# A spectral convolution kernel: exponent tables and mirror differences moved between stages and engines

## The chip, the cores and the metric

The kernel runs on one core of one Trainium2 chip. The metric is the device time of the whole program in microseconds; the three runs shown before the change have a median of 2677.54 us (2671.09 to 2678.12). Engines are named as in the profile: PE (TensorE, matrix products; PEld is its weight load), DVE (VectorE), ACT (ScalarE), POOL (GpSimd) and SP (SyncE, which here only issues transfers). [...]

## The reference, cut to what matters

The input x is 16 images of 16 channels, 256 x 256, in float32. Two layers follow each other, each a group normalization (`_gn`), a convolution and a residual sum:

```python
x = x + _L0_conv_ref(_gn(x), L0_conv_weight)          # 3x3 circular convolution
x = x + _L1_conv_ref(_gn(x), ty, tx, pole1, pole2, residue)

# _L1_conv_ref, cut
alpha = fft2(x)
A = 1 / (omega1 - pole1);  Bm = 1 / (omega2 - pole2)
S = einsum('ikpq,oikp,xikq->oxik', residue, A, Bm)
output_residue1 = einsum('biox,oxik->bkox', alpha, S)
output_residue2 = einsum('bikpq,ikpq->bkpq', D, residue)  # D: alpha with A and Bm
x1 = ifft2(output_residue1).real
E1 = exp(pole1[..., None] * ty);  E2 = exp(pole2[..., None] * tx)
F = einsum('kbpq,bipz->kbiqz', output_residue2, E1)
x2 = einsum('kbiqz,biqx->kizx', F, E2).real
return x1 + x2 / Nx / Ny
```

The exponentials E1 and E2 depend on the poles and coordinates only, not on x. They are wanted in the last stage alone, for x2.

## The kernel before, in words

The work goes through four stages, with all large intermediates in DRAM between them.

1. **Convolution** (lines 107 to 665, span 0 to about 618 us). A loop over g runs 384 steps and three more, 24 steps for each image b: `conv(g)` issues 32 small matmul records into four accumulators `ps_conv`. Every sixth step a pair of row groups is finished: ScalarE evicts it to `vt` (L280), and `mirror` (L230) then takes the two mirrored halves `lo` and `hi`, makes their sum in `vsum` (L232) and their difference in place in `lo` (L235), both on VectorE. `square` (L240) makes the squares with running sums on ScalarE, and SP stores sum and difference as `vD` (L292). The three lists `later`, `squared` and `folded` hold work back to a step number: mirror at g + 2, squares at g + 4 and g + 5, stores at g + 3, where g is the step of the last eviction of the pair. Statistics of x for the images ahead (`x_stats`: bn_stats on VectorE, small matmuls L178, weights `wc`) and x loads (L123, at steps 3 and 15 of an image) run in between.

   Two chains of generators make tables beside it, one piece every 2 or 4 steps: `make_poles`, `make_hat` twice and `make_c` on the one, `make_exps` twice and `make_coef` on the other.

   `make_exps(which)` makes E1 or E2 as real tables in eight pairs q. For a pair: `th` = t times the pole's imaginary part (GpSimd, L490), `ex` = Exp of t times its real part (ScalarE, L491), a rounding of the angle to turns with a large constant (`rn`, GpSimd, L492 to L495), the reduction of the angle in three steps (VectorE, L501) and clamping (L504, L505), Sin (ScalarE, L507), the product with `ex` and the sum and difference of mirrored halves (GpSimd, L509, L511), and the store to `eD` (SP, L516), twice for E1 and once for E2. Each alternation of Exp and Sin loads an activation table (ACT_TABLE_LOAD).

2. **Transform along y and x** (line 668 on, about 618 to 1243 us): v is read back, folded by VectorE and GpSimd, and multiplied with the tables; the spectrum goes to `aD`. Unchanged.

3. **Mixing** (lines 868 to 1131, about 1243 to 1910 us). For each of 32 groups g of frequencies and each of four steps n: `sums` (L981) makes the mixing weights for g + 1 into two banks `ps_s`; `spread` copies each bank into `sg`, half by ScalarE (L996) and half by VectorE's stream_shuffle (L997); `mix` (L1063) makes four banks `ps_mix`, three emptied into `yt` by ScalarE and the fourth by VectorE (both L1120). `load(g + 1, n)` then fetches the part of `aD` for the next g (nothing for n = 0; L1045 for n = 1; L1050 for n = 2, 3), and `store(g, n, yt)` (L1077) writes four transfers to `yD`. There are two `yt` buffers. `weights` (L918) prepares the factors for g + 2 in three pieces on VectorE (L926 to L942), and for a last product `w` on GpSimd (L952), in the step n = 2.

4. **Inverse transform and output** (line 1134 on, about 1910 to 2677 us): reads `yD`, `eD` (`et`, `ey`) and v, and writes the result. Unchanged.

Within a stage the order on each engine is the order of the code (`manual_schedule`). A pool with one buffer (`bufs` 1) lets a tile of the same tag be written again only when its last reader, a transfer included, is done.

Of the kernel before, what the change touches and what calls it, by code (L numbers as in the profile page):

```python
# [17 lines left out]
C = 16  # L18
# [6 lines left out]
def conv_then_laplace_kernel(ctx: ExitStack, tc: tile.TileContext, a: dict, out: bass.AP):  # L25
# [84 lines left out]
    vp = p1.enter_context(tc.tile_pool(name="vt", bufs=4))  # L110
# [119 lines left out]
    def mirror(g, b, u, lo, hi):  # L230
        both = fp.tile([P, 2, 2, N], FP, name="vsum", tag="vsum")
        nc.vector.scalar_tensor_tensor(  # L232
            both, lo, 1.0, hi, ALU.mult, ALU.add, accum_out=sums[:, b, u : u + 1]
        )
        nc.vector.tensor_tensor(lo, lo, hi, ALU.subtract)  # L235
        folded.append((g + 3, b, u, (both, lo)))
        squared.append((g + 4, lambda: square(both, 4 + 2 * u, b, bias=shift2[:, b : b + 1])))
        squared.append((g + 5, lambda: square(lo, 5 + 2 * u, b)))
# [211 lines left out]
    def make_coef():  # L450


        rs = sw.tile([P, C, 4, 2], FP, name="s_rs", tag="s_th")
# [3 lines left out]
        u = sw.tile([P, 4, C, 4], FP, name="s_u", tag="s_rn")  # L457
# [14 lines left out]

    def make_exps(which):


        pl = sw.tile([P, C, 2], FP, name="s_pl", tag="s_pl")
        nc.sync.dma_start(out=pl, in_=a[f"pole_e{which + 1}"])
        t = sw.tile([P, N], FP, name="s_t", tag="s_t")
        nc.sync.dma_start(out=t, in_=a[("ty", "tx")[which]].to_broadcast([P, N]))
        sign, phase, turns = (cols[:, 2 + 3 * which + j : 3 + 3 * which + j] for j in range(3))  # L480
        pim = sw.tile([P, C], FP, name="s_pim", tag="s_pim")
        nc.vector.tensor_scalar(pim, pl[:, :, 1], sign, None, ALU.mult)
        yield
        for q in range(8):
            th = sw.tile([P, 2, N], FP, name="s_th", tag="s_th")
            rn = sw.tile([P, 2, N], FP, name="s_rn", tag="s_rn")
            ex = sw.tile([P, 2, N], FP, name="s_ex", tag=f"s_ex{q % 2}")
            for j in range(2):
                i = 2 * q + j
                nc.gpsimd.tensor_scalar(th[:, j], t, pim[:, i : i + 1], None, ALU.mult)  # L490
                nc.scalar.activation(ex[:, j], t, AF.Exp, scale=pl[:, i, 0:1])  # L491
            nc.gpsimd.tensor_scalar(rn, th, 1.0 / (2 * PI), turns, ALU.mult, ALU.add)  # L492
            magic = 1.5 * 2.0**23
            nc.gpsimd.tensor_scalar(rn, rn, magic, None, ALU.add)
            nc.gpsimd.tensor_scalar(rn, rn, magic, None, ALU.subtract)  # L495
            yield
            c1 = 6.28125
            c2 = float(np.float32(1.93500518798828125e-3))
            c3 = 2 * np.pi - c1 - c2
            for c in (c1, c2, c3):  # L500
                nc.vector.scalar_tensor_tensor(th, rn, -float(c), th, ALU.mult, ALU.add)  # L501
                if c == c2:
                    yield
            nc.vector.tensor_scalar(th, th, phase, 3.1415925, ALU.add, ALU.min)  # L504
            nc.vector.tensor_scalar(th, th, -3.1415925, None, ALU.max)  # L505
            yield
            nc.scalar.activation(th, th, AF.Sin)  # L507
            yield
            nc.gpsimd.tensor_tensor(th, th, ex, ALU.mult)  # L509
            for op, eo in ((ALU.add, 0), (ALU.subtract, 1)):  # L510
                nc.gpsimd.tensor_tensor(  # L511
                    ex[:, :, eo * P : eo * P + P], th[:, :, 0:P], th[:, :, N - 1 : P - 1 : -1], op
                )
            yield
            for o in range(2 - which):
                nc.sync.dma_start(  # L516
                    out=eD[which][o, :, 2 * q : 2 * q + 2].rearrange("p i e t -> p i (e t)"),
                    in_=ex,
                )
# [114 lines left out]
    for b in range(1, B):  # L634
# [4 lines left out]
        (4, 1, chain(make_exps(0), make_exps(1), make_coef())),  # L639
# [234 lines left out]
    kp0 = pool(p2, "spare")  # L874
# [19 lines left out]
    kp0.tile([P, 2304], FP, name="spare", tag="spare")  # L894
# [208 lines left out]

    p2.enter_context(tc.manual_schedule())
# [3 lines left out]
    unmix = None  # L1108
    for g in range(32):
# [3 lines left out]
        for n in range(4):  # L1113
            evict = sums(n, w_now) if ahead is not None else []
            yt = yp.tile([P, 2, 4 * B, 16], FP, name="yt", tag="yt")
            for odd, ps in enumerate(evict):
                spread(ahead, n, odd, ps.rearrange("p q n -> p n q"))
            for m in range(4):
                o, src = mix(4 * n + m, sg, yt)
                (nc.vector.tensor_copy if m == 3 else nc.scalar.copy)(o, src)  # L1120
            if g < 31:
                load(g + 1, n)
            store(g, n, yt)
            if n == 1 and unmix is not None:
                next(unmix, None)
                unmix = None
            wt = next_step(steps, None) or wt
        if g == 2:
            unmix = unmix_first()
            next(unmix)  # L1130
    p2.close()
# [360 lines left out]
```

## Time and profile before

| | |
|---|---|
| median of 3 runs | 2677.54 us |
| profiled execution, its own time | 2679.43 us |
| its span | 2677.6 us |
| mean granted TensorE clock | 0.982 |
| busy: PE, PEld, DVE, ACT, POOL | 2508.3, 1861.7, 2029.9, 1480.2, 1014.6 us |
| chain that ended last, by engine | PE 59%, DVE 12%, DMA 11%, POOL 5%, issue 5%, ACT 4%, SPq 4% |
| groups of the chain | ps_mix L1063 11%, ps_y L730 9% and L738 8%, DMA yD<-yt 4%, ps_conv L265 4% |
| ACT COPY yt L1120 (384) | busy 203.9 us, idle before it 214.8 us |
| DVE differences L235 (64) | busy 89.2 us, mean 1393 ns |
| POOL w L952 (32) | busy 60.9 us, idle before it 534.0 us |

Busy time is the union of an engine's instructions. A group's idle time is what its engine did nothing in before these instructions, with the releaser that ended most of it. The chain is followed backward from the last instruction, at each step to what released it. The granted clock and the transfer share (mean busy share of the 16 DMA engines) are given for each stretch in the tables by windows.

### The profile page before, as it was taken

How to read it: one execution, taken by the hardware profiler on the slowest of the kernel's cores; microseconds unless marked ns; L12 is line 12 of the kernel's file. 1: busy time of each engine (PE TensorE's matmuls, PEld its weight loads, DVE VectorE, ACT ScalarE, POOL GpSimd, SP SyncE). 2: the span in 40 equal slices, each digit the busy share in tenths (PEclk: the TensorE clock that was granted, in tenths of full speed). 3: DMA queues.
4: the chain of work that ended last, by engine and by line, in shares of the span. 5: the costliest groups of instructions: out<-in, count | busy, mean ns of one | idle time of the engine just before them, and what ended most of it. 6: DMA issues, size and time to landing. Idle time of an engine off the chain costs nothing.

```text
span 2677.6 us, 84178 instructions
## 1 busy us (share of the span) xinstructions
PE 2508.3 (94%) x35376; PEld 1861.7 (70%) x35376; DVE 2029.9 (76%) x3774; ACT 1480.2 (55%) x2772; POOL 1014.6 (38%) x988
## 2 busy tenths in 40 slices
PE   5888899898999999997989999999799999999998
PEld 2333444455777777774778888888678888888887
DVE  7777798967888888887777878787267666766666
ACT  4666687775666666664545555566334444444443
POOL 1333476612333333333200101010456565565753
PEclk9999999998999999998999999999899999999999
DMA  8777688855665666565667777777789899898995
GB/s 302 263 270 247 239 302 280 285 194 174 240 223 204 215 238 220 203 221 206 188 199 217 226 220 229 219 229 222 220 285 290 282 288 284 285 290 286 291 287 179
DMA packets 462729, 652.23 MB, mean 244 GB/s; under 512 B 49336, under 2 KB 425144, under 8 KB 448400
## 3 DMA queue, kind: packets, MB, share of 16 engines
q1 hardware_dynamic: 461280, 639.65, 73.6%
q8 instruction: 279, 4.57, 0.7%
q0 software_dynamic: 928, 3.02, 0.4%
q10 hardware_dynamic: 144, 4.19, 0.4%
q14 instruction: 98, 0.80, 0.1%
HBM read 367.22 MB, written 279.50 MB: 242 GB/s over the span
## 4 chain that ended last, share of the span: by engine, by line
PE 59%; DVE 12%; DMA 11%; POOL 5%; issue 5%; ACT 4%; SPq 4%; DVEq 0%; ACTq 0%; POOLq 0%
PE ps_mix L1063 11%; PE ps_y L730 9%; PE ps_y L738 8%; PE ps_p L1246 6%; PE ps_f L1270 5%; PE ps_f L1271 5%; PE ps_x L773 4%; DMA yD<-yt 4%; PE ps_conv L265 4%; PE ps_s L981 3%; DMA out_y<-ol 3%; DMA yk<-yD 2%; DVE xst L166 2%; SPq L1077 2%; DVE r L1279 2%
## 5 line engine op out<-in xcount | busy, mean ns | idle before, releaser
L1063 PEld LDWEIGHTS ps_mix<-abd,sg 128*64 128x64 f32 x8192 | 450.9, 138 | 74.3 <-ACT yt L1120 55.8
L1063 PE MATMUL ps_mix<-abd,sg 128*64 128x128 f32 x8192 | 481.9, 276 | 20.8 <-ACT yt L1120 20.6
L265 PE MATMUL ps_conv<-xt,wc 32*32 32x512 f32 x12288 | 459.0, 608 | 28.9 <-issue 17.7
L1210 POOL TENSOR_TENSOR u<-yk 128x512 f32<-128x512 f32 (+1 forms) x268 | 348.4, 1331 | 311.1 <-PE ps_p L1246 197.8
L746 ACT ACTIVATE t<-ps_y,vmr 128x384 f32<-128x384 f32 x512 | 298.1, 582 | 158.9 <-PE ps_y L738 158.8
L265 PEld LDWEIGHTS ps_conv<-xt,wc 32*32 32x32 f32 x12288 | 223.1, 104 | 216.7 <-issue 127.6
L997 DVE STREAM_SHUFFLE sg<-ps_s 128x512 f32<-128x512 f32 (+1 forms) x264 | 326.0, 1325 | 0.0
L1120 ACT COPY yt<-ps_mix 128x512 f32<-128x512 f32 x384 | 203.9, 600 | 214.8 <-DMA yD<-yt 174.5
L730 PE MATMUL ps_y<-tabE,vq 128*128 128x256 f32 x1024 | 313.5, 388 | 9.4 <-DVE vq L719 7.8
L738 PE MATMUL ps_y<-tabO,vq 128*128 128x256 f32 x1024 | 306.3, 381 | 0.0
L1270 PE MATMUL ps_f<-pt,inv 128*128 128x256 f32 x1008 | 300.6, 380 | 0.0
L1271 PE MATMUL ps_f<-hs,ey 128*128 128x256 f32 x1008 | 299.8, 379 | 0.0
L1246 PEld LDWEIGHTS ps_p<-inv,u 128*128 128x128 f32 x2048 | 265.6, 193 | 42.2 <-issue 24.7
L1274 DVE TENSOR_TENSOR r<-ps_f,q 128x256 f32<-128x256 f32 x256 | 107.0, 418 | 246.6 <-ACT q L1273 246.6
L1246 PE MATMUL ps_p<-inv,u 128*128 128x128 f32 x2048 | 279.1, 280 | 4.9 <-POOL u L1214 4.9
L952 POOL TENSOR_TENSOR w<-v,mcol 128x1024 f32<-128x1024 f32 x32 | 60.9, 1902 | 534.0 <-DVE v L942 534.0
L1273 ACT COPY q<-ps_f 128x256 f32<-128x256 f32 x256 | 95.6, 373 | 286.3 <-PE ps_f L1271 284.1
L730 PEld LDWEIGHTS ps_y<-tabE,vq 128*128 128x128 f32 x1024 | 189.8, 191 | 85.9 <-ACT q L786 50.3
L280 ACT ACTIVATE vt<-ps_conv,xq 128x512 f32<-128x512 f32 x256 | 160.6, 683 | 117.1 <-PE ps_conv L265 116.6
L1248 ACT COPY pt<-ps_p 128x512 f32<-128x512 f32 x256 | 150.5, 588 | 130.7 <-PE ps_p L1246 126.1
L738 PEld LDWEIGHTS ps_y<-tabO,vq 128*128 128x128 f32 x1024 | 195.7, 191 | 27.0
L1271 PEld LDWEIGHTS ps_f<-hs,ey 128*128 128x128 f32 x1008 | 191.5, 190 | 26.0
(232 smaller groups left out, 3822.6 us busy)
## 6 DMA issues: line engine op xcount, KB each, us to landing
xt<-in_x SPq DMA_DIRECT2D x31, 2322.0 KB, 9.6
yD<-yt SPq DMA_DIRECT2D x512, 128.0 KB, 3.2
vl<-vD SPq DMA_DIRECT2D x256, 256.0 KB, 3.8
out_y<-ol SPq DMA_DIRECT2D x128, 512.0 KB, 9.8
s<-vD SPq DMA_DIRECT2D x252, 256.0 KB, 6.4
aD<-spec SPq DMA_DIRECT2D x15, 4096.0 KB, 12.6
yk<-yD SPq DMA_DIRECT2D x60, 1024.0 KB, 8.3
vD<-vsum SPq DMA_DIRECT2D x128, 256.0 KB, 4.5
```

Source lines behind the costliest of these rows:

```text
L265: nc.tensor.matmul(acc[r][32 * c : 32 * c + 32], lhsT=ready[b][0][rows, phase, tap], rhs=halves[b][u // 2][rows, q : q + 5 : 4, 2 - tap : ...
L280: nc.scalar.activation(vt[:, r % 2], acc[r], AF.Identity, bias=ready[b][1])
L730: nc.tensor.matmul(ps[:, 0:N], lhsT=vf[:, xo, 0, j], rhs=tabE[:, 0 : i + 2 : i + 1], start=True, stop=False, skip_group_check=True,)
L738: nc.tensor.matmul(ps[:, P : P + N], lhsT=vf[:, xo, 1, j], rhs=tabO[:, i : C + 1 : C - i], start=False, stop=True, skip_group_check=True,)
L746: nc.scalar.activation(t[:, xo, j].rearrange("p l n -> p (l n)"), ps[:, 0:384], AF.Copy, scale=vmr[:, 0, b0 + j, i : i + 1],)
L997: nc.vector.stream_shuffle(to[..., C + k : C + k + 2], src, swap)
L1063: nc.tensor.matmul(ps[64 * t : 64 * t + 64, j], lhsT=sg[:, f : f + 2].rearrange("p f m -> p (f m)"), rhs=abd[jq][:, :, 2 * t + cc, 2 * jj ...
L1120: (nc.vector.tensor_copy if m == 3 else nc.scalar.copy)(o, src)
L1210: nc.gpsimd.tensor_tensor(u[:, :, j].rearrange("p b (c n) -> p c b n", c=8), in0, in1, o)
L1246: nc.tensor.matmul(ps[:, at], lhsT=u[:, n], rhs=tab, start=True, stop=True)
L1270: nc.tensor.matmul(ps[:, e], lhsT=tab, rhs=pt[:, e], start=True, stop=False)
L1271: nc.tensor.matmul(ps[:, e], lhsT=ey[:, e], rhs=hs, start=False, stop=True)
```

## The change

Three things are done.

- In `mirror` the difference of the halves goes from VectorE to GpSimd. The square of the sum is queued at g + 5 in place of g + 4, that of the difference at g + 7 in place of g + 5, and the stores of both at g + 6 in place of g + 3. The pool of `vt` has six buffers in place of four.
- `make_exps` leaves the convolution and runs in the mixing stage, one piece a step from g = 1 on. Its work on VectorE (three angle steps, clamping and the small product `pim`) is now on GpSimd, where a fused multiply and add becomes a product in `tmp` and a subtraction. All its tiles, `ex` among them, have one buffer, in a pool that stands where a spare tile stood. It has one more `yield`, after the store. `make_coef` alone remains in the second chain of the convolution, with tags of its own.
- In the mixing stage a step's `store` is issued before the next group's `load`.

```diff
-    vp = p1.enter_context(tc.tile_pool(name="vt", bufs=4))
+    vp = p1.enter_context(tc.tile_pool(name="vt", bufs=6))
...
-        nc.vector.tensor_tensor(lo, lo, hi, ALU.subtract)
-        folded.append((g + 3, b, u, (both, lo)))
-        squared.append((g + 4, lambda: square(both, 4 + 2 * u, b, bias=shift2[:, b : b + 1])))
-        squared.append((g + 5, lambda: square(lo, 5 + 2 * u, b)))
+        nc.gpsimd.tensor_tensor(lo, lo, hi, ALU.subtract)
+        folded.append((g + 6, b, u, (both, lo)))
+        squared.append((g + 5, lambda: square(both, 4 + 2 * u, b, bias=shift2[:, b : b + 1])))
+        squared.append((g + 7, lambda: square(lo, 5 + 2 * u, b)))
...
-        (4, 1, chain(make_exps(0), make_exps(1), make_coef())),
+        (4, 1, make_coef()),
...
-    kp0 = pool(p2, "spare")
+    ep = pool(p2, "exps")
...
+    def make_exps(which):
+        pl = ep.tile([P, C, 2], FP, name="s_pl", tag="s_pl")
+        nc.sync.dma_start(out=pl, in_=a[f"pole_e{which + 1}"])
+        t = ep.tile([P, N], FP, name="s_t", tag="s_t")
+        nc.sync.dma_start(out=t, in_=a[("ty", "tx")[which]].to_broadcast([P, N]))
...
+        nc.gpsimd.tensor_scalar(pim, pl[:, :, 1], sign, None, ALU.mult)
+        yield
+        for q in range(8):
...
+            ex = ep.tile([P, 2, N], FP, name="s_ex", tag="s_ex")
+            for j in range(2):
+                i = 2 * q + j
+                nc.gpsimd.tensor_scalar(th[:, j], t, pim[:, i : i + 1], None, ALU.mult)
+                nc.scalar.activation(ex[:, j], t, AF.Exp, scale=pl[:, i, 0:1])
+            nc.gpsimd.tensor_scalar(rn, th, 1.0 / (2 * PI), turns, ALU.mult, ALU.add)
+            magic = 1.5 * 2.0**23
+            nc.gpsimd.tensor_scalar(rn, rn, magic, None, ALU.add)
+            nc.gpsimd.tensor_scalar(rn, rn, magic, None, ALU.subtract)
+            yield
...
+            for c in (c1, c2, c3):
+                nc.gpsimd.tensor_scalar(tmp, rn, float(c), None, ALU.mult)
+                nc.gpsimd.tensor_tensor(th, th, tmp, ALU.subtract)
+                if c == c2:
+                    yield
+            nc.gpsimd.tensor_scalar(th, th, phase, 3.1415925, ALU.add, ALU.min)
+            nc.gpsimd.tensor_scalar(th, th, -3.1415925, None, ALU.max)
+            yield
+            nc.scalar.activation(th, th, AF.Sin)
+            yield
+            nc.gpsimd.tensor_tensor(th, th, ex, ALU.mult)
+            for op, eo in ((ALU.add, 0), (ALU.subtract, 1)):
+                nc.gpsimd.tensor_tensor(
+                    ex[:, :, eo * P : eo * P + P], th[:, :, 0:P], th[:, :, N - 1 : P - 1 : -1], op
+                )
+            yield
+            for o in range(2 - which):
+                nc.sync.dma_start(
+                    out=eD[which][o, :, 2 * q : 2 * q + 2].rearrange("p i e t -> p i (e t)"),
+                    in_=ex,
+                )
+            yield
...
+    exps = chain(make_exps(0), make_exps(1))
     for g in range(32):
...
+            store(g, n, yt)
             if g < 31:
                 load(g + 1, n)
-            store(g, n, yt)
...
             wt = next_step(steps, None) or wt
+            if g:
+                next(exps, None)
...
+    for _ in exps:
+        pass
```

More of the change, by code (lines that the diff above doesn't have):

```diff
@@ L450, in make_coef @@
     def make_coef():
-        rs = sw.tile([P, C, 4, 2], FP, name="s_rs", tag="s_th")
+        rs = sw.tile([P, C, 4, 2], FP, name="s_rs", tag="s_rs")
         nc.sync.dma_start(out=rs, in_=a["res_kq"])
@@ L456, in make_coef @@
         yield
-        u = sw.tile([P, 4, C, 4], FP, name="s_u", tag="s_rn")
+        u = sw.tile([P, 4, C, 4], FP, name="s_u", tag="s_u")
         m0, m1 = cols[:, 0:1], cols[:, 1:2]
@@ L471, in make_coef @@
         yield
[L473 to L519, printed above, removed]
     def make_c():
@@ L893, in conv_then_laplace_kernel @@
     ]
-    kp0.tile([P, 2304], FP, name="spare", tag="spare")
     zp.tile([P, 384], FP, name="between", tag="between")
@@ L1100, in unmix_first @@
             nc.sync.dma_start(out=at[:, c], in_=t[:, c])
+    def make_exps(which):
[3 more added lines that the diff above has]
+        nc.sync.dma_start(out=t, in_=a[("ty", "tx")[which]].to_broadcast([P, N]))
+        sign, phase, turns = (cols[:, 2 + 3 * which + j : 3 + 3 * which + j] for j in range(3))
+        pim = ep.tile([P, C], FP, name="s_pim", tag="s_pim")
+        nc.gpsimd.tensor_scalar(pim, pl[:, :, 1], sign, None, ALU.mult)
+        yield
+        for q in range(8):
+            th = ep.tile([P, 2, N], FP, name="s_th", tag="s_th")
+            rn = ep.tile([P, 2, N], FP, name="s_rn", tag="s_rn")
+            tmp = ep.tile([P, 2, N], FP, name="s_tmp", tag="s_tmp")
+            ex = ep.tile([P, 2, N], FP, name="s_ex", tag="s_ex")
[8 more added lines that the diff above has]
+            yield
+            c1 = 6.28125
+            c2 = float(np.float32(1.93500518798828125e-3))
+            c3 = 2 * np.pi - c1 - c2
+            for c in (c1, c2, c3):
[20 more added lines that the diff above has]
+            yield
```

## The prediction

> **What bounds the kernel now.** First the busy time by stage; the stages end where ps_conv, ps_y and ps_mix end.
>
> ```profile
> core 0: us, PE busy (x) PEld busy (x) DVE busy (x) ACT busy (x) POOL busy (x), PEclk, DMA share, GB/s
> 0.00:618.00 618.00, 524.16 (x12708) 257.75 (x12708) 486.77 (x896) 415.69 (x693) 272.00 (x256) 0.97 0.77 265
> 1243.00:1910.00 667.00, 623.81 (x12459) 521.89 (x12460) 503.20 (x977) 366.02 (x671) 83.94 (x47) 0.97 0.73 214
> ...
> 26.20:350.00 323.80, 278.17 (x6369) 131.18 (x6370) 251.85 (x465) 211.36 (x338) 132.79 (x109) 0.96 0.77 258
> 350.00:450.00 100.00, 95.59 (x2510) 47.52 (x2507) 96.01 (x161) 83.50 (x146) 69.25 (x70) 1.00 0.88 307
> 450.00:613.40 163.40, 148.23 (x3858) 77.57 (x3827) 123.20 (x232) 116.07 (x202) 69.77 (x75) 0.98 0.69 238
> ```
>
> In the convolution (first row, and the last three in pieces) no engine is full. From 26.2 to 613.4 PE idles 65 us: 46, 4 and 15 in the three pieces. Between 350 and 450 it is nearly full already although VectorE is full too, so there is little to win there. In the mixing stage PE is busy 94%. The chain of waits gives PE's own pace in both stages (start, duration, what, count):
>
> ```profile
> 581.04 20.07 PE ps_conv L265 x573
> ...
> 1460.81 3.65 PE ps_mix L1063 x64
> 1465.48 3.64 PE ps_mix L1063 x64
> ```
>
> At 32 records a step the first line is 17.9 convolution steps of 1.12 us. In the mixing stage one step's ps_mix follows the last by 4.67 us, 3.65 of its own and 1.0 of ps_s, so 128 steps make 598 us. Its first ps_mix begins at 1280 and the last copy of yt ends at 1908; about 28 us of that are stalls.
>
> Next the waits of the mixing stage, then its SP queue and a piece of the convolution's timeline (start, duration, engine, line).
>
> ```profile
> POOL w L952 <- DVE v L942: 534.0, 32, 27.6
> ACT yt L1120 <- DMA yD<-yt: 174.5, 78, 8.9
> DVE sg L997 <- ACT sg L996: 80.2, 124, 1.5
> ...
> 1558.04 1.96 SPq L1077 DMA_DIRECT2D yD<-yt  x4
> 1560.09 3.40 SPq L1050 DMA_DIRECT2D abd<-aD  x4
> 1563.61 5.56 SPq L1077 DMA_DIRECT2D yD<-yt  x8
> ...
> 156.71 1.90 POOL L509 TENSOR_TENSOR s_th<-s_th,s_ex 128x512 f32<-128x512 f32 x1 [12.93 <-ACT s_th L507]
> 157.57 1.06 DVE L187 TENSOR_TENSOR xq<-xq 128x1 f32<-128x1 f32 x1
> 158.66 0.76 DVE L188 SCALAR_TENSOR_TENSOR xq<-xq 128x1 f32<-128x1 f32 x1
> 158.69 1.41 POOL L511 TENSOR_TENSOR s_ex<-s_th 128x256 f32<-128x256 f32 x2
> ```
>
> GpSimd has 534 us of free time in the mixing stage. ScalarE looks idle, but 174.5 us of that is waiting for a yt buffer whose store has not landed, and VectorE's shuffle waits for ScalarE in each step: a late ScalarE makes VectorE late. SP issues stores in about 2.0 us a step and loads in 2.5, 3.1 and 3.4 us in three steps of four, so it is busy 17 of 18.7 us. The last four lines show a one-column VectorE instruction (usually 0.16 us) lasting until GpSimd's ends.
>
> **What the Trainium skill says.** "SBUF — State Buffer" (§ SBUF: two separate sides) has a VectorE instruction with two SBUF inputs and a GpSimd instruction that reads SBUF exclude each other, the later one blocked for the whole instruction. The timeline agrees: L187 ends at 158.63, L509 at 158.61. "GPSIMD Engine Reference" (§ Performance versus the Vector engine) puts a two-input elementwise instruction at about twice VectorE; here 1.27 us against 0.69 (L718). "ScalarE: Activation LUTs" (§ What ACT_TABLE_LOAD costs) gives 1283 ns plus a drain of 1380; the trace shows the 1283, but the next instruction starts 1.3 us after, so I count no drain.
>
> **The change, part by part.**
>
> *Convolution, removed.* VectorE loses 48 x 0.739 (L501) + 16 x (0.501 + 0.446) (L504, L505) = 51 us and the 64 differences (L235), 89 us: 487 becomes 347. ScalarE loses 32 table loads of 1.283, 32 Exp of 0.503 (L491, 14.6 busy as they overlap) and 16 Sin of 0.632: 66 us. GpSimd loses 157 us (L490, L492, L494, L495, L509, L511). SP loses 24 eD issues of 0.48.
>
> *Convolution, added.* 64 differences of 1024 elements on GpSimd. Not shown there; 256 elements take 0.73 us and 512 take 1.27, so 1024 take 2.4 us, bounds 2.3 and 3.0 (the slope from L509's 1.53). 154 us, which leaves GpSimd where it was. Its difference is 2.4 us late where VectorE's was 1.2, but square and store of that tile come two and three steps (of 1.5 us) later than before, and six vt buffers pay for the longer hold. Sums stay on VectorE.
>
> *Convolution, gain.* PE's 65 us by releaser: VectorE (L174, L188, L211 and others) 28, ScalarE (vt, tabE, tabO, hB) 16, GpSimd (s_num) 5, "issue" 18, 67 with the records that overlap. With VectorE down by 29% and ScalarE by 16% I take 80% of the first, 60% of the second, nothing of the third and 45% of the last, 22 + 10 + 8 = 40 us. Lower bound 10: the transfers (share 0.77) have to follow, and each x load now stands right behind a store of 1 MB. Upper bound 75: PE's own work is 384 steps of 1.12 (573 records in 20.07 us, 32 a step) plus 68 us of small matmuls, 498 of the 587 us, and some stall hides inside "busy". At the end one more square and a GpSimd difference stand before the next stage: 2 us, at most 9 if the first load of s, on POOL's queue, falls behind the last difference.
>
> *Mixing, the swap.* Store before load: a store is issued about 3 us earlier in three steps of four, SP's sum is unchanged. Of the 28 us of stalls some 5 are at the end, 5 come from unmix_first taking a yt buffer and 3 from a lower clock. I take the rest but 2: 13 us gained, bounds 0 and 25.
>
> *Mixing, Exp.* From g = 1 each step runs one piece of the generator: six pieces for a pair of exponentials (GpSimd and Exp; GpSimd; GpSimd; Sin; GpSimd; eD store), 98 of 124 steps in all. There is one ex buffer, so the Exp of a pair waits on ScalarE until the eD store of the pair before has landed, and the spreads and yt copies queue behind it. Count from PE's end of the step in which the store is issued, loads of jq 2: yD store from 0.75 to 2.75, loads to 5.85, two eD issues to 6.8, landing 3.3 later, 10.1. ScalarE arrives at 4.67 - 0.3 = 4.4, so it waits 5.7; with table load and two Exp (2.3) it is blocked 8.0 us. PE meanwhile does a whole step and the next ps_s (5.7 us), then needs a bank that ScalarE empties 1.9 us after it resumes: the stall is blocked time minus 4.1, 3.9 us. Six steps on jq has moved by two. With jq 0 there are no loads, but SP comes 1.2 us late from the steps before: landing at 8.2, blocked 6.1, stall 2.0. In the second table, with one store, jq 3 lands at 10.4 (stall 4.2) and jq 1 at 9.0 (2.9). The first pair of each table waits for nothing: 4 x 3.9 + 3 x 2.0 + 4 x 4.2 + 3 x 2.9 = 47 us. Bounds 20 and 70.
>
> *Mixing, Sin.* GpSimd needs for a pair, by medians, 5.5 + 5.8 + 5.1 + 3.0 us in its four pieces, 19.4 in six steps of 28, with 1.9 for each w between. Since w waits for v of its own step, GpSimd can't run ahead, and Sin waits 0 to 4 us; with 1.9 of its own it passes the 4.1 us only at times: 5 us, bounds 0 and 30.
>
> *Mixing, the port pair.* GpSimd is then busy some 70% of the time, in instructions of 1.2 us. Seven two-input VectorE instructions of weights (L926, L932, L933, L937, L938, L941, L942) come in bursts of 3, 2 and 2. If every burst met a busy GpSimd: half an instruction for the first, a whole one for each other, 6.6 us, 4.6 at 70%. The convolution's small instructions show about half of what this sum gives for them (L188: mean 0.38, median 0.22). Half is 2.3 us for each g; VectorE has 18.7 - 8 x 1.36 - 4 x 0.70 - 3.0 = 2.0 us free for each g, but not always at the right place, and the shuffles it is late with gate the next g. I take 0.8 us x 25 g = 20 us, bounds 0 and 90.
>
> Moved eD stores add 12 us of issue and 6.3 MB; they are in the Exp sum. The rest of the queue (poles and t, four loads) and make_coef's two own buffers cost nothing: SP idles in the step without loads. The y and final stages keep their 625 and 767 us.
>
> **Sum.** Convolution -40, junction +2, mixing 47 + 5 + 20 - 13 = +59: +21 us. The profiled execution took 2679.4 (span 2677.6), the median is 2677.5, 0.1% lower; +21 on it is 2699.
>
> **Rivals.** (a) Faster: ScalarE's 215 us of idle time before the yt copies takes the exponentials in. Place: the Exp behind the eD store; price 47 us; it decides once the store lands within 6.2 us of PE's end of step (blocked time under 4.1), since then neither PE nor the shuffles are held. For: idle time, and the swap, which frees the queue. Against: SP's order above. Mixing +12 then: 2677.5 - 40 + 2 + 12 = 2652. (b) The convolution doesn't speed up, PE or the transfers being its bound as between 350 and 450: gain 10, 2677.5 - 10 + 2 + 59 = 2729. Against: the stalls before 350. (c) It cancels: no port waits and no Sin waits, mixing +34, 2677.5 - 40 + 2 + 34 = 2674, no change within the scatter.
>
> **Chances.** Forecast 0.54, (a) 0.12, (b) 0.22, (c) 0.12. 0.3%, 8 us, is about what a measurement can tell. Slower: 0.50 of the forecast's, all of (b), 0.04 of (c): 0.76. Same: 0.03 + 0.05 = 0.08. Faster: 0.01 + 0.12 + 0.03 = 0.16. Bounds of the forecast's terms, taken as independent, make about 35 us either way; with (b) and half of (a) the range is 2645 to 2750.
>
> **What would show it.** The conv stage ends near 575 instead of 613, PE's waits on xq almost gone. In the mixing stage: Exp waiting for DMA eD<-s_ex, 4 to 6 us each; w or th of POOL and weights on VectorE longer than before (L926 above 0.28 us); DMA yD<-yt before the yt copies well under 174. I am wrong if ex has landed when Exp comes, or if the convolution gains 60 us or more.

## The result and the profile after

The changed kernel takes 2783.9 us (median of 4 runs, 2777.32 to 2789.08) beside 2676.09 us before (4 runs, 2671.09 to 2678.12): slower, ratio 1.0404, 95% interval 1.0377 to 1.0432. The forecast was 2699 in a range of 2645 to 2750. The direction was right; the cost was not 21 us but about 108.

The profiled execution has a span of 2782.5 us at a mean granted clock of 0.966 (before 2677.6 at 0.982). By stages:

| from ... to | before, us | after, us |
|---|---|---|
| first to last ps_conv | 587.1 | 560.2 |
| last ps_conv to first ps_y | 8.4 | 12.2 |
| first to last ps_y | 615.9 | 615.4 |
| last ps_y to first ps_mix | 42.5 | 42.3 |
| first ps_mix to first ps_p | 636.9 | 762.5 |
| first to last ps_p | 746.6 | 749.6 |

So the convolution gave 27 us, 4 of them were lost before the y stage, and the mixing stage took 126 more. The 3 us of the last row lie within what that stage varies by in all the runs below (741 to 750 us). The same windows as before the change, the convolution in its three pieces and then the mixing stage from its first ps_mix to its last copy of yt:

```profile
core 0: us, PE busy (x) PEld busy (x) DVE busy (x) ACT busy (x) POOL busy (x), PEclk, DMA share, GB/s
26.20:350.00 323.80, 295.99 (x6847) 147.51 (x6852) 208.36 (x440) 175.33 (x308) 117.80 (x75) 0.96 0.79 262
350.00:450.00 100.00, 93.39 (x2390) 44.38 (x2376) 62.55 (x124) 61.01 (x116) 55.76 (x51) 1.00 0.83 282
450.00:586.40 136.40, 129.23 (x3492) 72.39 (x3474) 78.17 (x151) 90.48 (x169) 69.93 (x58) 1.00 0.69 239
1256.00:2009.00 753.00, 637.91 (x12136) 543.49 (x12136) 477.42 (x874) 421.63 (x710) 386.66 (x297) 0.93 0.67 191
```

In the convolution PE's idle time fell from 65 us to 28 + 7 + 7 = 42. In the mixing stage PE's idle time is now 115 us of 753, and the clock is 0.93, where the stage had 0.99 before (1280 to 1908). VectorE's busy time there is 477, as before (475).

The waits of the mixing stage (engine and line, what it waited for, us in total, times, longest):

```profile
POOL w L903 <- DVE v L893: 258.9, 28, 19.0
DVE sg L948 <- ACT sg L947: 211.8, 80, 8.7
...
ACT L1074 <- DMA eD<-s_ex: 86.1, 14, 6.9
PE ps_mix L1014 <- ACT yt L1123: 74.2, 25, 5.4
...
ACT s_th L1091 <- POOL s_th L1089: 44.1, 9, 6.7
...
ACT yt L1123 <- DMA yD<-yt: 29.3, 16, 6.2
```

The third and fifth lines are the two new waits on ScalarE: Exp behind the store of `ex` (14 of 16 pairs, 6.2 us each), Sin behind GpSimd (9 times, 4.9 us each). The second and fourth show who pays: VectorE's shuffle behind ScalarE's half of `sg` (80 us before), and PE before banks that ScalarE hasn't emptied. The last line was 174.5 us before.

One Sin and one Exp in the timeline, ScalarE first (start, duration, engine, line, operation, [idle before it, released by]):

```profile
1524.89 1.28 ACT L1091 ACT_TABLE_LOAD   x1
1532.00 0.63 ACT L1091 ACTIVATE s_th<-s_th 128x512 f32<-128x512 f32 x1 [5.83 <-POOL s_th L1089]
...
1551.19 1.28 ACT L1074 ACT_TABLE_LOAD   x1 [5.65 <-DMA eD<-s_ex]
1552.48 0.91 ACT L1074 ACTIVATE s_ex<-s_t,s_pl 128x256 f32<-128x256 f32 x2
```

The table load of a Sin doesn't wait with it: it is done by 1526.2, and the 5.83 us of waiting come after it. That of an Exp comes after the wait. TensorE in the same stretches:

```profile
1526.07 3.71 PE L1014 MATMUL ps_mix<-abd,sg 128*64 128x128 f32 x64
1529.71 1.09 PE L932 MATMUL ps_s<-ct,w 64*32 64x256 f32 x32
1534.31 6.80 PE L1014 MATMUL ps_mix<-abd,sg 128*64 128x128 f32 x64 [3.51 <-ACT yt L1123]
...
1555.07 6.50 PE L1014 MATMUL ps_mix<-abd,sg 128*64 128x128 f32 x64 [3.59 <-ACT yt L1123]
...
1562.52 3.71 PE L1014 MATMUL ps_mix<-abd,sg 128*64 128x128 f32 x64
```

The idle time is what the prediction's formula gives: ScalarE is blocked for 5.65 + 1.28 + 0.91 = 7.8 us at the Exp, minus 4.1 is 3.7 (3.59 measured). But the 64 matmuls after each stall take 6.5 to 6.8 us in place of 3.71. The windows of that stretch say why (the granted clock, PEclk, is the third number from the end):

```profile
1534.00:1537.00 3.00, 2.64 (x22) 2.24 (x24) 3.00 (x5) 2.97 (x6) 1.42 (x2) 0.50 0.00 0
1537.00:1541.00 4.00, 4.00 (x46) 3.87 (x42) 3.00 (x7) 1.17 (x2) 0.00 (x0) 0.58 0.86 188
1541.00:1545.00 4.00, 4.00 (x89) 3.42 (x88) 3.12 (x7) 2.38 (x5) 2.60 (x2) 1.00 0.96 318
```

After an idle stretch of 3.5 us the granted clock is 0.50 for 3 us and 0.58 over the next 4. "TensorE: Matmul & The Clock Gate" of the Trainium skill (Part 1: The HAM clock gate) has it that about 3.4 us of idle time put the clock to half, and that about 3.4 us of sustained work bring it back. Here 3.5 us of idle time did it, which agrees; but some 6 us of work passed before the clock was back (by estimate: 3 us at half clock, and 3.4 us more if the 4 us at a mean of 0.58 are part half and part full clock), which is longer. Stalls shorter than 3.4 us can do it too, as the sections on the half clock and on what was not expected show. The stall of 3.5 us costs 6.6: 3.51 of idle time, and 6.80 in place of 3.71 for the matmuls.

GpSimd before that Sin:

```profile
1517.57 1.89 POOL L903 TENSOR_TENSOR w<-v,mcol 128x1024 f32<-128x1024 f32 x1 [12.93 <-PE ps_mix L1014]
1519.55 1.49 POOL L1084 TENSOR_SCALAR s_tmp<-s_rn 128x512 f32<-128x512 f32 x1
1521.13 1.28 POOL L1085 TENSOR_TENSOR s_th<-s_th,s_tmp 128x512 f32<-128x512 f32 x1
...
1528.39 2.01 POOL L1088 TENSOR_SCALAR s_th<-s_th,cols 128x512 f32<-128x512 f32 x1
1530.48 1.49 POOL L1089 TENSOR_SCALAR s_th<-s_th 128x512 f32<-128x512 f32 x1
```

GpSimd had stood 12.9 us before `w` (the profile names a ps_mix as what ended it, in 28 other cases `v`); then two pieces of the angle's reduction run back to back, from 1519.6 to 1532.0, and ScalarE waits from 1526.2 on.

### The profile page after: what moved, and what is told of

Read it like the earlier page. It is cut to its first block, busy times and chain, and to the rows that moved or that the text cites. A ratio compares the mean times of both kernels' runs of the same rounds, so it can differ in the third digit from the quotient of the medians.

```text
span 2782.5 us, 84304 instructions
## 1 busy us (share of the span) xinstructions
PE 2541.9 (91%) x35376; PEld 1901.6 (68%) x35376; DVE 1911.7 (69%) x3628; ACT 1463.7 (53%) x2758; POOL 1306.4 (47%) x1182
## 5 line engine op out<-in xcount | busy, mean ns | idle before, releaser
L1014 PE MATMUL ps_mix<-abd,sg 128*64 128x128 f32 x8192 | 517.4, 288 | 108.0 <-ACT yt L1123 74.2
L1014 PEld LDWEIGHTS ps_mix<-abd,sg 128*64 128x64 f32 x8192 | 483.2, 145 | 165.6 <-ACT yt L1123 98.8
L265 PEld LDWEIGHTS ps_conv<-xt,wc 32*32 32x32 f32 x12288 | 232.8, 104 | 214.2 <-issue 154.7
L235 POOL TENSOR_TENSOR vt<-vt 128x1024 f32<-128x1024 f32 x64 | 152.4, 2381 | 327.9 <-DVE vsum L232 255.0
L1123 ACT COPY yt<-ps_mix 128x512 f32<-128x512 f32 x384 | 215.3, 590 | 99.8 <-PE ps_mix L1014 53.5
L670 POOL TENSOR_TENSOR vq<-vf 128x512 f32<-128x512 f32 x64 | 81.4, 1272 | 293.7 <-DVE vf L674 276.4
L947 ACT ACTIVATE sg<-ps_s,mcol 128x512 f32<-128x512 f32 (+1 forms) x264 | 166.9, 686 | 91.1 <-PE ps_s L932 90.8
```

Source lines behind the costliest of these rows:

```text
L265: nc.tensor.matmul(acc[r][32 * c : 32 * c + 32], lhsT=ready[b][0][rows, phase, tap], rhs=halves[b][u // 2][rows, q : q + 5 : 4, 2 - tap : ...
L947: nc.scalar.activation(to[..., k : k + 2], src, AF.Copy, scale=nsgn)
L1014: nc.tensor.matmul(ps[64 * t : 64 * t + 64, j], lhsT=sg[:, f : f + 2].rearrange("p f m -> p (f m)"), rhs=abd[jq][:, :, 2 * t + cc, 2 * jj ...
```

## The experiments

All times are medians; a ratio is to the kernel before, run beside it on the same chip. "Stretch" is from the first ps_mix to the first ps_p in the profiled execution: 636.9 us before, 762.5 after. A single execution's stretch is good to some 5 us only, since executions of one kernel differ by 10 us and more.

### Parts of the change undone: ScalarE's waits

**swap_only**: the kernel before with the store ahead of the load.

```diff
+            store(g, n, yt)
             if g < 31:
                 load(g + 1, n)
-            store(g, n, yt)
```

> The kernel before with one part of the change: a step's store is issued ahead of the next group's load. The prediction put this at 13 us gained (0 to 25). All theories agree on the sign; if the order on SP was what made ScalarE wait, its wait for yD<-yt (174.5 us before) falls below 60 us and the time is about 2663 us. If the landing of the stores is bound by the transfers themselves, the wait stays above 120 us and the time at 2676 us.

Measured 2673.12 us (12 runs), ratio 0.9993, 0.9976 to 1.001: no gain, although both readings of the expectation had the wait decide the time. Its waits in the mixing stage:

```profile
ACT yt L1120 <- DMA yD<-yt: 60.5, 40, 10.7
DVE yt L1120 <- DMA yD<-yt: 30.5, 8, 10.5
PE ps_mix L1063 <- DMA abd<-aD: 10.8, 11, 2.2
```

The swap did what it says: the first wait fell from 174.5 to 60.5 us. But PE's idle time before ps_mix went from 20.8 to 32.1 us: the loads of `abd`, now behind a store that waits for the last copy of yt, come late 11 times, and 8.2 us of PE's idle time lie at the very end, before the last ps_mix. The stretch is 642.0. Most of ScalarE's wait had not held PE: with 114 us less of it, PE's own wait for the copies of yt fell by 4 us only, from 20.6 to 16.8.

**ex_out**: the changed kernel, in which the final sum and difference go to `tmp` and the store to `eD` reads `tmp`, so that the next Exp waits for no store.

```diff
-                    ex[:, :, eo * P : eo * P + P], th[:, :, 0:P], th[:, :, N - 1 : P - 1 : -1], op
+                    tmp[:, :, eo * P : eo * P + P], th[:, :, 0:P], th[:, :, N - 1 : P - 1 : -1], op
...
-                    in_=ex,
+                    in_=tmp,
```

> The changed kernel, but the last sum and difference go to tmp and the eD store reads tmp, so that ex is free as soon as GpSimd has multiplied with it, and ScalarE's Exp waits for no store (GpSimd waits instead, a step later). Theory 'blocked ScalarE': the 14 waits of 86 us and the 63 us of PE idle time behind them go, with some 27 us of slow clock; Sin may wait a little longer as steps get shorter: 2700 to 2725 us. Rival 'GpSimd and the port pair': GpSimd does the same work at the same places, so 2765 us or more. Rival 'amount of work on ScalarE' (67 us of Exp, Sin and table loads): unchanged work, 2765 us or more.

Measured 2731.55 us (4 runs), ratio 1.0236, 1.019 to 1.0283; stretch 716.7. Without the wait for the store behind Exp the kernel takes 52 us less (46 by the stretch). The waits of Sin grew at the same time, from 9 of 44.1 us to 15 of 69.4 us: part of what Exp no longer loses may be lost at Sin.

**ex_out_sin**: ex_out with one more `yield` before Sin.

```diff
             nc.gpsimd.tensor_scalar(th, th, -3.1415925, None, ALU.max)
             yield
+            yield
             nc.scalar.activation(th, th, AF.Sin)
```

> As ex_out, and Sin comes one step later, so that GpSimd has its angle ready. Theory 'blocked ScalarE': with neither Exp nor Sin waiting, a block is only 1.9 or 2.3 us, under the 4.1 us that PE stands; PE's idle time in the mixing stage falls from 105 us to under 35, its clock stays up, and the kernel takes 2640 to 2670 us, less than before the change. Rival 'GpSimd and the port pair': 2750 us or more. Rival 'amount of work on ScalarE': 2720 us or more.

Measured 2681.74 us (20 runs), ratio 1.0034, 1.0017 to 1.0051; stretch 661.2. One line took another 50 us away (56 by the stretch). The expected 2640 to 2670 was missed: with both waits gone the stretch is still some 25 us above the 636.9 of before.

**sin_late**: that `yield` alone, on the changed kernel.

> The changed kernel with one more step between the GpSimd work on th and the Sin, so that ScalarE doesn't wait for th; Exp still waits for the store of ex. Theory 'both blocks cost by themselves': the same 50 us as this step brought beside the free ex buffer, 2725 to 2745. Rival 'one hides the other': ScalarE's waits at Exp make the room in which GpSimd's delay at Sin is lost anyhow; 2765 to 2785. The prediction's 5 us for Sin would give 2779.

Measured 2740.01 us (4 runs), ratio 1.0245, 1.0208 to 1.0283: 44 us below the changed kernel. The two waits cost by themselves; one does not hide the other. Sin's wait costs 44 us beside that of Exp and 50 without it, Exp's 58 and 52. The stretch is 728.9, 34 us shorter; the rest of the 44 lies mainly in the convolution (550.7 us in this profiled execution, 560.2 in the changed kernel's), whose code is the same. So Sin's cost is known to within some 10 us only. Sin's waits are down to 4 of 6.5 us together, PE's idle time before ps_mix fell from 108.0 to 82.4, and its busy time there from 517.4 to 506.0.

**keep_warm**: the changed kernel with the ps_s matmuls repeated in the second step after an Exp or Sin block (31 steps).

```diff
-            evict = sums(n, w_now) if ahead is not None else []
+            evict = sums(n, w_now, 4 if did[-2] else 1) if ahead is not None else []
...
-            if g:
-                next(exps, None)
+            did.append(next(exps, None) if g else None)
```

> The changed kernel, in which the 32 ps_s matmuls of a step are issued four times over (same bank, same values, some 3.4 us more of TensorE) in the steps that come second after an Exp or a Sin block, where TensorE otherwise stands idle for 3 to 6 us. The result is unchanged. Theory 'half clock': the idle time itself is only part of the loss, the matmuls after it run at about half clock for some 4 us; with the idle stretch filled the clock stays, and the time falls by 20 to 40 us, to 2745 to 2765. Rival 'idle only': the added matmuls only fill time that is lost anyhow; 2780 to 2800.

Measured 2786.12 us (4 runs), ratio 1.0406, 1.0372 to 1.044: the expected 20 to 40 us did not come. Its two groups in the mixing stage (line, engine, operation, count, busy us, mean ns, idle before):

```profile
L1014 PE MATMUL ps_mix<-abd,sg 128*64 128x128 f32 x8192 | 497.4, 281 | 53.1 <-ACT yt L1124 20.7 <-ACT sg L947 12.7 <-DMA abd<-aD 11.9
L932 PE MATMUL ps_s<-ct,w 64*32 64x256 f32 x7166 | 228.1, 383 | 8.6 <-DVE other L948 4.7 <-POOL w L903 3.8
```

The changed kernel has:

```profile
L1014 PE MATMUL ps_mix<-abd,sg 128*64 128x128 f32 x8192 | 517.4, 288 | 108.0 <-ACT yt L1123 74.2
```

The repeats added 76 us to ps_s (152.3 before). 55 of them filled idle time before ps_mix, and there the clock held: ps_mix is busy 20 us less. The other 21 us came where PE had work, and took the gain back. So filling part of the idle time took 20 us of slow matmuls away, but the experiment's total doesn't show a gain, since it paid as much as it saved. The 35 us between 517.4 and the 481.9 of before remain the best estimate of what slow matmuls cost in all.

### What stays when ScalarE waits for nothing

**pool_only**: ex_out without Exp and Sin; GpSimd multiplies with `rn` in the place of `ex`, so that the exponential and the sine are left out of the tables.

```diff
-                nc.scalar.activation(ex[:, j], t, AF.Exp, scale=pl[:, i, 0:1])
...
-            nc.scalar.activation(th, th, AF.Sin)
...
-            nc.gpsimd.tensor_tensor(th, th, ex, ALU.mult)
+            nc.gpsimd.tensor_tensor(th, th, rn, ALU.mult)
```

> As ex_out, without ScalarE's Exp and Sin (GpSimd multiplies with rn in the place of ex, so E1 and E2 are left out of the result): all of GpSimd's instructions stay, none of ScalarE's. Theory 'blocked ScalarE' and rival 'amount of work on ScalarE': the mixing stage is as good as without the exponentials, 2630 to 2655 us in all. Rival 'GpSimd and the port pair': the loss stays, 2750 us or more, with VectorE's two-input instructions of weights above 0.5 us.

Measured 2680.37 us (20 runs), ratio 1.0031, 1.0018 to 1.0043; stretch 661.2, as ex_out_sin. Neither range was met, the theory's 2630 to 2655 or the rival's 2750. So ScalarE's work costs nothing that can be seen once it doesn't wait, and the 25 us are not ScalarE's.

**no_exps**: no arithmetic for the tables at all; the stores send one zeroed tile.

```diff
+        tmp = ep.tile([P, 2, N], FP, name="s_tmp", tag="s_tmp")
+        nc.gpsimd.memset(tmp, 0.0)
```

> The changed kernel with the whole computation of the two tables left out (one tile is set to zero and the twenty-four table stores of the mixing stage send it, so the output is not the reference's). It leaves the convolution, the order of store and load and the table stores as the change made them, and takes away ScalarE's and GpSimd's work in the mixing stage. Theory 'GpSimd': what still costs some 25 us in the mixing stage once ScalarE waits for nothing is GpSimd's arithmetic, which makes the weights w late; then this kernel keeps the convolution's gain of 23 us and runs at 2650 to 2660. Rival 'order': the swap of store and load and the extra table stores cost those 25 us; then it runs at 2672 to 2682.

Measured 2679.72 us (20 runs), ratio 1.0011, 0.9994 to 1.0028. As measured, hardly any of the 25 us went with GpSimd's work. But 9 us of the result are this kernel's own: the load of the tile `ct` came late (last ps_y to first ps_s 23.7 us in place of 14.6; why is not shown, the pool of the tables is smaller here). In no_stores, below, with the pool at full size, it is 14.7 again. Without the 9 us it would be about 2671, 10 us below pool_only. y_mix_full, below, is the cleaner comparison: the same 24 stores in this stage, no arithmetic, no late `ct`, and 2670.39, also 10 us below pool_only. That is what GpSimd's arithmetic costs.

**no_exps_dve**: no_exps with the difference on VectorE and the old lags.

```diff
-        nc.gpsimd.tensor_tensor(lo, lo, hi, ALU.subtract)
-        folded.append((g + 6, b, u, (both, lo)))
+        nc.vector.tensor_tensor(lo, lo, hi, ALU.subtract)
+        folded.append((g + 3, b, u, (both, lo)))
```

> As no_exps (tables left out), with the mirror difference back on VectorE and the lags of the squares and of the stores of v as before the change; six vt buffers stay. Theory 'tables': the convolution's gain comes from the tables' work having left VectorE and GpSimd, and the difference on GpSimd adds little; then within 5 us of no_exps. Rival 'difference': the gain comes from VectorE's relief by the difference (48 of 1.7 us); then 15 to 25 us above no_exps, and the last ps_conv at about 605 to 613 us.

Measured 2671.02 us (12 runs), ratio 0.9987, 0.9967 to 1.0006, with the same late `ct`. The convolution took 556.8 us (563.7 in no_exps, 550.7 to 560.7 in the other kernels with the difference on GpSimd), and the y stage followed after 8.3 us in place of 12.7. The time is 9 us below no_exps, in neither range of the expectation. The difference on GpSimd brings the convolution nothing that can be seen and costs 4 us at its end. The convolution's gain comes from the rest of what the change did there. That is argued to be the tables' leaving; but every run without the tables in the convolution also has six `vt` buffers and `make_coef` alone in its chain, so that the share of these two isn't separated.

**no_stores**: as no_exps, the pool at its full size, and the stores of zeros sent from the y stage.

```diff
+    ep.tile([P, 2352], FP, name="spare", tag="spare")
...
+        if 8 <= u < 56 and u % 2 == 0:
+            x = (u - 8) // 2
+            which, o, q = (0, x // 8, x % 8) if x < 16 else (1, 0, x % 8)
+            nc.sync.dma_start(
+                out=eD[which][o, :, 2 * q : 2 * q + 2].rearrange("p i e t -> p i (e t)"),
+                in_=zero[:, 0:512].rearrange("p (i x) -> p i x", i=2),
+            )
```

> As no_exps (the tables' computation left out, zeros in their place), but the twenty-four stores of 256 KB leave in the y stage, so that the mixing stage holds nothing of the tables at all; it keeps the swap of store and load. Theory 'table stores': the 6 MB, 5 per cent more transfer in a stage whose transfer engines are busy for three quarters of the time, cost 10 to 15 us there; then from the first ps_mix to the first ps_p it takes 640 to 644 us, as with the swap alone (642.0), and the time is 2646 to 2658. Rival 'swap': the late loads of abd cost it whatever else is in the stage; 653 to 660 us for that stretch, time 2660 to 2672.

Measured 2646.48 us (4 runs), ratio 0.9876, 0.9843 to 0.991; stretch 631.0 (640 to 644 were expected). This is the missing piece: without the table stores the mixing stage is as short as before.

**y_mix_full** and **y_mix_small**: no_stores with 24 more stores in the mixing stage, at the changed kernel's places, of 256 KB (first below) and of 64 KB (second).

```diff
+                    nc.sync.dma_start(
+                        out=eD[which][o, :, 2 * q : 2 * q + 2].rearrange("p i e t -> p i (e t)"),
+                        in_=z2.rearrange("p (i x) -> p i x", i=2),
+                    )
```

```diff
+                    nc.sync.dma_start(out=eD[which][o, :, 2 * q, 0], in_=z2[:, 0:128])
```

> no_stores (tables left out, zeros stored in the y stage) with twenty-four more stores of 256 KB of zeros in the mixing stage, where the change has its table stores. Both theories ('bytes' and 'number'): 15 to 30 us above no_stores, 2662 to 2676. If it stays below 2655, the stores are not what no_stores took away.

> As y_mix_full, at the same places, but each of the twenty-four stores has 64 KB. Theory 'bytes': a quarter of what y_mix_full adds, 4 to 8 us above no_stores, 2650 to 2655. Theory 'number': SP's issue and the loads of abd behind it cost the same whatever the size, within 6 us of y_mix_full.

Measured 2670.39 us (20 runs; ratio 0.9983, 0.9971 to 0.9995) and 2661.35 us (4 runs; 0.9942, 0.9924 to 0.9961): 24 and 15 us above no_stores. ps_mix in no_stores and in y_mix_full:

```profile
L1022 PE MATMUL ps_mix<-abd,sg 128*64 128x128 f32 x8192 | 475.9, 274 | 21.5 <-DMA abd<-aD 12.5 <-ACT yt L1081 7.1 <-ACT sg L955 0.9
```

```profile
L1022 PE MATMUL ps_mix<-abd,sg 128*64 128x128 f32 x8192 | 482.1, 276 | 34.7 <-DMA abd<-aD 16.2 <-ACT yt L1096 8.4 <-DVE sg L956 4.5
```

By the stretch (650.6 in y_mix_full) the stores cost 20 us, spread over many small waits (13 us more, with no single releaser) and 6 us of slower matmuls. Neither theory holds alone: a quarter of the bytes costs about 60% of the time. Twenty-four stores in this stage's queue cost about 1 us each, by estimate 0.6 for being there and 0.4 for their size, in a stage whose transfer engines are busy three quarters of the time. That they cost something is clear: every execution of no_stores (up to 2647.2) is below every one with the small stores (from 2655.6). The split is not: the small stores' executions, up to 2665.0, reach into those of the full ones, from 2662.2, and the 64 KB stores also write 512 bytes a partition where the full ones write 2 KB.

### Towards a better version

**load_first**: ex_out_sin with the load ahead of the store again.

> The changed kernel with the free ex buffer and the later Sin (ex_out_sin), and the load of abd again ahead of the store of yt, as before the change. Theory 'swap costs': TensorE's waits for abd (12.7 us) go, those of ScalarE for the store of yt come back beside work that now has fewer gaps; 2665 to 2678. Rival 'swap pays': with the tables' work on ScalarE the waits for the store can no longer be absorbed, and it is the swap's gain of the prediction (13 us or more) that is lost; 2690 to 2715.

Measured 2679.98 us (12 runs), ratio 1.0011, 0.9994 to 1.0028; ex_out_sin is at 1.0034. PE's waits for `abd` are gone, those for ScalarE rise from 14.6 to 21.0 us. The order of store and load makes no difference to the time that is worth having in either kernel.

**best**: ex_out_sin with `v` made one step before `w`, the load ahead of the store in step n = 1 only, and two steps between the loads of the poles and t and their use.

```diff
         nc.vector.tensor_tensor(den, den, pr2, ALU.add)
-        yield
         nc.vector.reciprocal(den, den)
+        yield
...
         nc.vector.tensor_tensor(v[:, :, 1], f, den, ALU.mult)
+        yield
...
+            if g < 31 and n == 1:
+                load(g + 1, n)
             store(g, n, yt)
-            if g < 31:
+            if g < 31 and n > 1:
```

> ex_out_sin with three edits: the weights' v one step earlier, so that GpSimd doesn't stand waiting for it and w isn't late; the load ahead of the store in the second step of a group alone (the pair that the next group needs first); two steps between the loads of pl and t and their first use. Theory 'late w and abd': the 12 us of TensorE's waits for w, some 8 of the 13 for abd and 6 for t go; 2655 to 2668. Rival 'bound by transfers': the waits only change their name, since the stage's transfers set its length; 2674 to 2684.

Measured 2664.98 us (7 runs), ratio 0.9952, 0.9933 to 0.997: half a percent below the kernel before and 4% below the changed one. PE's waits for `w` on L903 fall from 11.8 us (6 times) to 2.6 (twice), those for `abd` vanish from its list, and those for ScalarE's copies of yt rise from 14.6 to 29.0. What each of the three edits gives was not measured.

**best_dve**: best, with the difference back on VectorE and the old lags.

> As best, with the mirror difference back on VectorE and the old lags. Theory 'the difference gives nothing': the convolution is as long as in best within 6 us, and the start of the y stage is 4 us earlier, since the last difference no longer holds up the loads of s on GpSimd's queue; 0 to 6 us below best. Rival: without it the convolution loses 10 us or more.

Measured 2663.84 us (10 runs), ratio 0.9948, 0.9926 to 0.997, level with best. Its convolution and mixing stage in the profiled execution, which took 2654.96 us:

```profile
26.00:580.70 554.70, 518.99 (x12703) 260.19 (x12702) 413.43 (x774) 328.29 (x591) 112.97 (x124) 0.98 0.80 265
1247.80:1884.00 636.20, 602.58 (x12156) 509.47 (x12160) 479.82 (x873) 420.61 (x713) 384.88 (x297) 0.99 0.76 226
```

All of the tables' work is still in the mixing stage (ScalarE 421, GpSimd 385 us), at a clock of 0.99 and with the convolution's gain kept. This keeps about 12 us of the 29 that no_stores shows to be there.

**exps_y**: the tables, stores included, in the y stage, two pieces for each unit.

> The tables' arithmetic (with the free ex buffer and the later Sin) and their stores in the y stage, two pieces for each unit, none of it in the mixing stage; the convolution as in the changed kernel. Theory 'transfers': the y stage's transfer engines take the 6 MB beside their work, and ScalarE's blocks of 2 us fall into its idle time; y stage 616 to 626 us, time 2646 to 2660. Rival 'full TensorE': TensorE is busy 99.7% there, so each block of ScalarE stops it at the three ps_y banks; y stage 640 us or more, time 2670 or more.

Measured 2817.84 us (4 runs), ratio 1.0534, 1.0512 to 1.0556, the slowest of all. The y stage took 779 us in place of 615. Its waits:

```profile
POOL vq L669 <- DVE vf L673: 112.4, 27, 7.9
PEld ps_y L681 <- POOL vq L670: 90.0, 23, 6.5
...
PE ps_y L681 <- POOL vq L670: 80.6, 21, 6.1
```

The rival named the wrong engine: it is not ScalarE that stops TensorE (7.2 us before ps_y) but GpSimd, which makes half of `vq` for each unit and has the tables' instructions queued ahead of it. In one place a piece of them ran from 806.7 to 814.5, `vq` right behind it, and TensorE waited 3.3 us for `vq`. Slow matmuls add to that: the granted clock in this stage is 0.92, in the changed kernel 1.00. The explanation by transfers isn't tested by this kernel, because the queue of GpSimd decides first.

## Why the prediction was wrong

Of the 87 us between +21 and +108 most are in two terms of the mixing stage: the wait of Sin, priced at 5 us and measured at 44 to 50, and the table stores, priced at nothing of their own and measured at 24. The convolution (13 us) and the swap (13 us) gave less than was counted, the port pair cost some 10 us less. The terms follow in the prediction's order, with the half clock and the stores put in.

**Convolution, -40 forecast, -27 measured.** The engines' relief was right: VectorE 349 us (347 forecast), the difference 2.38 us on GpSimd (2.4). The step that failed is "45% of the last", the idle time that the profile puts down to "issue". PE's waits by releaser in the convolution, before and then after:

```profile
PE ps_conv L265 <- issue: 17.7, 13, 2.5
PE ps_stat L178 <- DVE xq L188: 14.2, 8, 5.8
PE ps_conv L265 <- ACT vt L280: 10.8, 7, 6.3
```

```profile
PE ps_conv L265 <- issue: 31.9, 25, 5.2
PE ps_setup L557 <- POOL s_num L544: 6.2, 3, 3.0
```

The waits for VectorE and ScalarE went almost wholly (from 26 and 16 us to 1 and 0), some 9 us more than the 80 and 60% that were counted. But "issue" was to fall by 8 us and grew by 14, 22 us off, and the two together make the 13 us that are missing. What "issue" hides is not shown by these runs. With VectorE at 412 us in no_exps_dve the convolution was as short, so VectorE's load is not it.

**Junction (from the convolution to the y stage), +2 (0 to 9), +4 measured**, for the reason given: the first load of s stands with the last difference on GpSimd's queue, and the gap goes back to 8.3 us when it is on VectorE.

**Swap, -13, nothing measured.** The step took 13 of 28 us of PE's stalls (30, by 628 less 598) as due to the store's wait. swap_only removed 114 us of that wait on ScalarE, and late loads of `abd` took the place of the stalls.

**Exp, +47 (20 to 70), 52 measured.** The mechanism holds in the trace, and so does the formula "blocked time minus 4.1", within half a microsecond in eleven of the fourteen stalls; in three, where PE waited for `sg` and not for a bank, it comes out 1.4 us short. The waits were longer than forecast, 6.2 us in place of 5.7, 3.8 and the like. So the fourteen stalls add up to 63 us of idle time where the forecast's 47 is idle time alone, and the 64 matmuls behind each took 29 us more than at full clock, which the forecast left out. Undoing the wait gave only 52, with longer waits elsewhere (Sin's went from 44.1 to 69.4). That 47 and 52 are so near is luck. The first pair of each table didn't wait for nothing: its Exp waited 4.9 and 7.3 us for the load of t, which the prediction counted as free.

**Sin, +5 (0 to 30), 44 to 50 measured.** This is the step that failed most: "Sin waits 0 to 4 us". GpSimd's time for a pair was right (19.4 forecast, 20.0 measured: 320.8 us of its ten lines by 16). The step named the cause too, that `w` waits for `v`, but took the wait of Sin as 0 to 4 us, past the limit "only at times", without setting the pieces on their steps. `w` is queued in step n = 2, ahead of that step's piece of the angle. A pair has six steps and a group four, so in every second pair of the first table that piece and the next stand behind `w`, with Sin two steps after it: 10.9 us of GpSimd work by the prediction's own pieces, begun when `v` comes. These four pairs wait 5.1 to 6.7 us. With the table load ahead of the wait, and 0.63 us of Sin, ScalarE is blocked for 7.7 us in the one shown, well past 4.1. Then comes the half clock. The second table begins with one piece of its own, which shifts its pairs by a step: there only the last piece stands behind `w`, in every second pair, with Sin in the very next step, and four pairs wait 4.1 to 4.2 us, as here:

```profile
1726.05 0.63 ACT L1091 ACTIVATE s_th<-s_th 128x512 f32<-128x512 f32 x1 [4.11 <-POOL s_th L1089]
```

(`w` ran at 1717.5, 9.4 us after GpSimd had come free for it, and that piece from 1719.5 to 1726.0.) The ninth wait, 3.3 us, is the first pair of the second table. At the first four PE loses 15 us of idle time and 10 of slow matmuls; how the rest of the 44 to 50 comes about was not traced.

**Half clock, not in the sum.** ps_mix is busy 517.4 us for 481.9: 35 us, contained in the two terms above as measured. In the changed kernel the 64 matmuls after a stall of 3.0 us or more took 5.4 to 6.8 us in place of 3.71, 1.7 to 3.1 us on top of the idle time. Below that it goes either way: two stalls of 2.88 us left them at 3.71, and one of 2.75 did not.

```profile
1292.32 3.71 PE L1014 MATMUL ps_mix<-abd,sg 128*64 128x128 f32 x64 [2.88 <-ACT yt L1123]
1387.33 6.90 PE L1014 MATMUL ps_mix<-abd,sg 128*64 128x128 f32 x64 [2.75 <-ACT yt L1123]
```

**Table stores, counted at nothing beyond Exp, 24 measured.** "Moved eD stores add 12 us of issue and 6.3 MB; they are in the Exp sum": they are in it as what Exp waits for, but y_mix_full has neither Exp nor GpSimd work and still pays 24 us. The prediction had the row of SP's load (17 of 18.7 us a group) and the transfer share, and drew no cost from them.

**Port pair (VectorE and GpSimd shutting each other out), +20 (0 to 90); GpSimd's arithmetic as a whole about 10.** The exclusion that the prediction took from "SBUF — State Buffer" of the Trainium skill (SBUF: two separate sides) fits what is seen: one of the small VectorE instructions with two inputs, first in pool_only and then in no_exps, where GpSimd does no arithmetic for the tables, 522 ns on average against 292:

```profile
L884 DVE TENSOR_TENSOR u<-u,prU 128x128 f32<-128x128 f32 x30 | 15.6, 522 | 1.0
```

```profile
L884 DVE TENSOR_TENSOR u<-u,prU 128x128 f32<-128x128 f32 x30 | 8.8, 292 | 1.0
```

The seven instructions of weights together took 70.3 us in the changed kernel, 60.7 before: 10 us of VectorE time. How much of that TensorE felt is not shown; the 10 us of total time that GpSimd's arithmetic costs also hold the late `w` behind the tables' work.

The sum as measured: no_stores stands 29 below the kernel before (the convolution's 27 less 4, and 6 that swap or scatter may give), table stores +24, GpSimd +10, Sin +50, Exp +52, together +107. The parts come from runs that follow each other edit by edit, so the sum had to come near the 108; each is good to some 5 to 10 us. Rival (b)'s 2729 is nearer in its total only: it has the convolution gain 10 us, further off than the forecast's 40; (a) fell with the 86.1 us that Exp waited for its store; (c) named the two terms, port and Sin, as zero, and only the first was small.

## What to carry to other kernels

Work that is moved into another engine's free time brings its waits with it: ask for each moved instruction what stands ahead of it in its engine's queue and when that is released, not only how long the queue is; one more step between producer and consumer was worth 44 to 50 us here. A stall of TensorE is to be priced with the slow matmuls after it as soon as it passes 2 to 3 us: 3.51 us of idle time cost 6.6 here. And transfers that are moved into a stage whose transfer queue is nearly full (SP busy 17 of 18.7 us) cost time even where no single wait shows it: 24 stores cost 24 us.

## What the runs showed of the hardware that was not expected

- How long TensorE must idle until the clock drops isn't sharp: in the changed kernel 2.88 us did nothing twice and 2.75 us made the next 64 matmuls take 6.90 us, while in swap_only they took 5.38 us after 2.16 and 2.39 us, and 3.71 after 2.21. The 3.4 us quoted above are no safe bound here.
- GpSimd's instructions on 128x512 differ by form (means in the changed kernel's mixing stage): multiply and add with two scalars 0.69 us (L1075), one scalar operation 1.49 (L1084), add and min 2.01 (L1088).
- With a smaller pool in the mixing stage the load of `ct` came 9 us later (no_exps); why is not shown.
